# Float products of an attention stage as four column tiles of 32 outputs

## Chip, cores and metric

The kernel runs on one core of one Trainium2 chip. The metric is the device time of one launch in microseconds; the time before is the median of three runs. All data are float32, except the operands of the two 3x3 convolutions, which are 8-bit floats.

## What is computed

Two layers run one after the other on x of shape (4, 128, 128, 128), channels second. The first is a windowed attention with a convolutional feed-forward part:

```
tok = 16x16 regions of x, step 14, as rows of 128 channels
y = LN(tok);  q, k, v = split(y @ w_qkv)              # 4 heads of 32
o = softmax(q k^T / sqrt(32)) v                       # inside each region
xf = average over overlaps of (o @ w_out + b_out + tok)
y = LN(xf) @ w_p0 + b_p0                              # 128 -> 256
y = depthwise 5x5 (y);  y = gelu(gelu(batchnorm(y)))
x1 = y @ w_p2 + b_p2 + xf                             # 256 -> 128
```

The second is quantise, 3x3 convolution, batch normalisation, quantise, 3x3 convolution, batch normalisation, plus x1.

## The kernel before

**Stages.** The attention stage covers the layer norms, the attention, the projection to 256 channels and most of the depthwise convolution; it fills about the first 2240 us of the profiled span. A rest of the depthwise convolution follows, then the stage with the gelus, the second projection (L1228) and the first 3x3 convolution, and the last stage with the second 3x3 convolution (both at L1164). Engines are scheduled by hand: except on GpSimd, instructions run in the order in which the program issues them.

**Tiling of the attention stage.** The image rows are cut into 36 bands (4 images, 9 bands of 16 rows with a step of 14), and each band into 9 regions of 16x16 pixels. Channels lie on the 128 partitions. The outer loop runs over the bands `t`, the inner over the regions `j`. In each `j` the kernel issues, in this order:

- `scores(j)` (L784): per head, keys as weights of 32 rows and 128 columns, queries moving, then an exponential on ScalarE (L792);
- `values(j - 1)` (L847, L855): per head, values as weights of 128 rows and 32 columns, exponentials moving; then sums with a matrix of ones, also 32 columns wide. The four heads write to four groups of 32 PSUM partitions;
- side work, handed out by `beside(t)` in four lists: the variance of the layer norms (L377, ones of 32 columns as weights, four slices of pixels to four partition groups), the projections, and the depthwise convolution (`depthwise`, L600, weights of 40 rows and 32 columns, eight at a time);
- on every second `j`, `values_in(j)` (L770): pixels as weights of 128x128, the value part of `wqkv` moving with 128 columns. Up to four such products fill one PSUM tile `pm`, which ScalarE copies to `v` (L775).

**The projections.** `project` in `ln1_chunks` (L493) makes queries and keys of band `t + 1` or a later one: weights of 128x128, 512 or 384 pixels moving, evicted by ScalarE to `q` (L500) or `kr` (L498). `project` in `post_chunks` (L545) applies the output weights to the finished band `t - 1`, with its sum on VectorE (L546). `p0` (L561) makes the 256 channels in two halves, evicted by ScalarE to `y` (L566) and stored to DRAM for the depthwise convolution.

All of these share one PSUM pool `ps_m` of three buffers, named `pm`. The scores use a pool of two tiles and the values one tile of their own.

**Numbers of products in a run.** L493 and L561 run 288 products each, L545 144, L770 648. In the profile each float32 product leaves two MATMUL and two LDWEIGHTS records.

A second, safe form of the attention stage stands behind a flag that the program works out from the weights; it is not run with the inputs used here.

Of the kernel before, what the change touches and what calls it, by code (L numbers as in the profile page):

```python
# [14 lines left out]
P = 128  # L15
# [31 lines left out]
def layers(  # L47
# [29 lines left out]
    nc = tc.nc  # L77
# [44 lines left out]
    wqkv = const.tile([P, 3 * P], F32, name="wqkv")  # L122
    nc.sync.dma_start(out=wqkv, in_=w_qkv)
    g1, b1 = vector(ln1_g, "g1"), vector(ln1_b, "b1")
    wo = const.tile([P, P], F32, name="wo")
# [3 lines left out]
    wp0 = const.tile([P, 2, P], F32, name="wp0")  # L129
# [6 lines left out]
    with (  # L136
# [21 lines left out]
        for w in (wqkv, wp0.rearrange("p h m -> p (h m)")):  # L158
            n = w.shape[1]
# [25 lines left out]
    with ExitStack() as actx:  # L185
# [21 lines left out]
        xb, xr, yr, qs, kr, ob = {}, {}, {}, {}, {}, {}  # L207
# [218 lines left out]
        def store(out, in_):  # L426
            stores.append((out, in_))

        def flush(n, engine=nc.sync):
            for out, in_ in stores[:n]:  # L430
                engine.dma_start(out=out, in_=in_)
            del stores[:n]

        def rows_of(t, r, n):
            return t[:, r : r + n, :].rearrange("p r c -> p (r c)")

        def windows(a, n):

            a = a[:, : n * P]
            return bass.AP(a.tensor, a.offset, [a.ap[0], [STEP, NR], [P, n], [1, RS]])  # L440
# [10 lines left out]
        def row_blocks(t):  # L451
            return row_chunks(0 if bands[t][1] == 0 else 2, RS, LB)

        def load_ahead(t, n):

            if t + 1 < len(bands):
                nxt = row_blocks(t + 1)[n]
                xb[t + 1, nxt[0]] = load_rows(xp, "xt", t + 1, *nxt)

        def ln1_begin(t):  # L460
            b, i = bands[t]
            qs[t] = yp.tile([P, RS, P], F32, name="q")
            if i:
                nc.gpsimd.tensor_copy(rows_of(qs[t], 0, 2), rows_of(qs[t - 1], RS - 2, 2))
            for held, name in ((yr, "yr"), (kr, "kr")):
                held[t] = yp.tile([P, NR, RS, RS], F32, name=name)
                if i:
                    nc.gpsimd.tensor_copy(
                        held[t][:, :, 0:2, :], held[t - 1][:, :, RS - 2 :, :]
                    )  # L470

        def ln1_chunks(t, sel=None):

            chunks = []
            for at, (r, n) in enumerate(row_blocks(t)):
                held = {}
                squares, variance, deviation, spread, scaled = normalise(
                    lambda r=r, n=n: xb[t, r][:, : n * P], n * P, sel
                )

                def second(r=r, n=n, at=at, held=held, scaled=scaled):
                    held["xn"] = scaled()
                    load_ahead(t, at)
                    for hh in range(2):
                        nc.gpsimd.tensor_copy(
                            yr[t][:, :, r + hh * n // 2 : r + (hh + 1) * n // 2, :],
                            windows(held["xn"][hh], n // 2),
                        )

                def project(m, hh, r=r, n=n // 2, held=held):  # L490
                    r = r + hh * n
                    pm = ps_m.tile([P, 512], F32, name="pm")
                    nc.tensor.matmul(  # L493
                        pm[:, : n * P], wqkv[:, m * P : (m + 1) * P], held["xn"][hh],
                        start=True, stop=True,
                    )
                    if m:
                        nc.scalar.copy(kr[t][:, :, r : r + n, :], windows(pm, n))  # L498
                    else:
                        nc.scalar.activation(  # L500
                            rows_of(qs[t], r, n), pm[:, : n * P], AF.Identity, bias=qb
                        )

                chunks.append(
                    [squares, variance, deviation, spread, second]
                    + [lambda p=project, m=m, hh=hh: p(m, hh) for hh in range(2) for m in range(2)]
                )
            return chunks
# [12 lines left out]
        def finished(t):  # L521
            return row_chunks(0, RS if bands[t][1] == NR - 1 else STEP, LB)
# [5 lines left out]
        def post_chunks(t, sel=None):  # L528


            b, i = bands[t]
            chunks = []
            for at, (r, n) in enumerate(finished(t)):
                held = {}
                squares, variance, deviation, spread, scaled = normalise(
                    lambda n=n, held=held: held["xf"][:, : n * P], n * P, sel
                )

                def project(hh, r=r, n=n, at=at, held=held):
                    if hh == 0:  # L540
                        held["xf"] = xfp.tile([P, LB * P], F32, name="xf")
                    px = slice(hh * n // 2 * P, (hh + 1) * n // 2 * P)
                    pm = ps_m.tile([P, 512], F32, name="pm")
                    po = pm[:, : n // 2 * P]
                    nc.tensor.matmul(po, wo, rows_of(ob[t], r + hh * n // 2, n // 2), start=True, stop=True)  # L545
                    nc.vector.scalar_tensor_tensor(  # L546
                        held["xf"][:, px], po, bo, xr[t, at][:, px], ALU.add, ALU.add
                    )
                    if hh:
                        store(  # L550
                            xf_d[b][:, (i * STEP + r) * P : (i * STEP + r + n) * P],
                            held["xf"][:, : n * P],
                        )

                def second(held=held, scaled=scaled):
                    held["xn"] = scaled()

                def p0(h, hh, r=r, n=n // 2, held=held):
                    row = i * STEP + r + hh * n
                    pm = ps_m.tile([P, 512], F32, name="pm")  # L560
                    nc.tensor.matmul(  # L561
                        pm[:, : n * P], wp0[:, h, :], held["xn"][hh], start=True, stop=True
                    )
                    y = y2t[h].pop(0)
                    y2t[h].append(y)
                    nc.scalar.activation(  # L566
                        y[:, :n],
                        pm[:, : n * P].rearrange("p (r c e) -> p r e c", r=n, e=2),
                        AF.Identity, bias=bp0[:, h : h + 1],
                    )  # L570
                    store(
                        y2_d[b][row + 2 : row + n + 2, :, h * P : (h + 1) * P, :].rearrange(
                            "r e p x -> p (r e) x"
                        ),
                        y[:, :n].rearrange("p r e x -> p (r e) x"),
                    )

                chunks.append(
                    [lambda p=project: p(0), lambda p=project: p(1), squares, variance, deviation, spread, second]
                    + [lambda p=p0, h=h, hh=hh: p(h, hh) for hh in range(2) for h in range(2)]  # L580
                )
            return chunks
# [166 lines left out]
        def attention(t):  # L749
# [11 lines left out]
            def region(src, j):  # L761
                return src[t][:, j].rearrange("p r c -> p (r c)")

            def values_in(j):

                two = range(j, min(j + 2, NR))
                pv = ps_m.tile([P, 2, 2, P], F32, name="pm")
                for m in range(len(two)):
                    for c in range(2):
                        nc.tensor.matmul(  # L770
                            pv[:, m, c, :], region(yr, j + m)[:, c * P : (c + 1) * P], wqkv[:, 2 * P :],
                            start=True, stop=True,
                        )
                v = attn_v.tile([P, 2, 2, P], F32, name="v")
                nc.scalar.copy(v[:, : len(two)], pv[:, : len(two)])  # L775
                for m in range(len(two)):
                    S["v", j + m] = v[:, m]
# [99 lines left out]
            if safe:  # L877
                return scores_safe, lambda j: None, values_in, values
            return scores, halves, values_in, values

        def beside(t, sel=None):
# [180 lines left out]
    with (  # L1062
# [20 lines left out]
        for m in range(2):  # L1083
            for h in range(2):
# [3 lines left out]
                    start=True, stop=True,  # L1088
# [274 lines left out]
def conv_seq_kernel(tc: tile.TileContext, *args: bass.AP):  # L1363
    nc = tc.nc
    with tc.tile_pool(name="flag", bufs=1) as fp:
        flag = fp.tile([1, 1], mybir.dt.int32, name="flag")
        layers(tc, False, flag, *args)


        large = nc.values_load(flag[0:1, 0:1])  # L1370
        with tc.If(large > 0):
            layers(tc, True, flag, *args)
# [34 lines left out]
```

## Time and profile before

| | |
|---|---|
| median of three runs | 3264.07 us (3260.51 to 3272.7) |
| span of the profiled execution | 3262.4 us |
| mean granted TensorE clock | 0.965 |
| TensorE busy (MATMUL) | 3089.8 us |
| TensorE weight loads busy | 1544.8 us |
| VectorE, ScalarE, GpSimd busy | 2018.7, 1991.5, 837.6 us |
| instructions | 75,716 |
| moved by DMA | 680.65 MB, mean 209 GB/s |

The profiled execution is a run of its own; its span runs from its first to its last instruction, and lies 1.7 us under the median of the timed runs. The matmul and weight-load records of TensorE are listed as two rows, PE and PEld. A matmul's end is modelled, so that a record's length holds some time after its stream: the distance between the starts of two records says more than the length of one. "Idle before" is time in which an engine had nothing running; a releaser is what ended it. A weight shape is given as rows*columns.

### The profile page before, as it was taken

To read this page: it belongs to the slowest core of one execution; us is meant where nothing else is said; L and a number is where in the kernel's file an instruction comes from. 1 tells how busy PE (TensorE), PEld (TensorE's weight loads), DVE (VectorE), ACT (ScalarE), POOL (GpSimd) and SP (SyncE) were. 2 spreads that over 40 slices of the span, in tenths; PEclk is the share of its full clock that TensorE was granted. 3 is DMA by queue.
4 is the path that set the end of the run, shared out by engine and by line. 5 is a ranking of instruction groups with operands and counts; after the bars stand their busy time and mean duration, and the time that the engine had idled before them with its cause. 6 is when DMAs were issued, how large, how long until landed. Compare 5 with 4: busy or idle time off the path is not lost.

```text
span 3262.4 us, 75716 instructions
## 1 busy us (share of the span) xinstructions
PE 3089.8 (95%) x30954; PEld 1544.8 (47%) x30954; DVE 2018.7 (62%) x3244; ACT 1991.5 (61%) x2658; POOL 837.6 (26%) x1058
## 2 busy tenths in 40 slices
PE   8999999999999999999989998876899999999998
PEld 4555554544544444544444444443544444444443
DVE  5877887776766667676655564542555555666543
ACT  5777776777776776767655564532467777433443
POOL 3444443333333333333322232211111111000000
PEclk9999999999999999999999998877699999999999
DMA  3555677888886888886889988857899999552398
GB/s 82 150 165 159 170 185 183 192 210 198 208 200 160 193 202 204 197 209 166 188 203 207 201 199 187 191 158 199 245 359 358 357 359 306 169 167 84 106 357 312
DMA packets 809828, 680.65 MB, mean 209 GB/s; under 512 B 580919, under 2 KB 695936, under 8 KB 809472
## 3 DMA queue, kind: packets, MB, share of 16 engines
q1 hardware_dynamic: 798879, 669.17, 75.6%
q8 instruction: 247, 4.05, 0.5%
q0 software_dynamic: 1024, 3.93, 0.4%
q10 hardware_dynamic: 9568, 2.61, 0.3%
q14 instruction: 110, 0.89, 0.1%
HBM read 408.72 MB, written 270.79 MB: 208 GB/s over the span
## 4 chain that ended last, share of the span: by engine, by line
PE 80%; DMA 7%; issue 4%; ACT 4%; SPq 3%; DVE 3%; POOL 0%; ACTq 0%; DVEq 0%; POOLq 0%
PE pc L1164 21%; PE pm L600 9%; PE sc L784 9%; PE po L847 8%; PE pm L493 7%; PE pb L1228 7%; PE pm L561 5%; PE pm L770 4%; PE po L855 4%; DMA y_d<-y 3%; PE pm L377 3%; PE pm L545 3%; ACT pt L792 2%; DVE rd L867 1%; DMA u<-y_d 1%
## 5 line engine op out<-in xcount | busy, mean ns | idle before, releaser
L867 DVE RECIPROCAL rd<-po 128x256 f32<-128x256 f32 x324 | 569.3, 1757 | 447.6 <-PE po L855 444.7
L792 ACT ACTIVATE pt<-sc 128x1024 f32<-128x1024 f32 x648 | 628.0, 1024 | 128.2 <-PE sc L784 62.6
L1164 PE MATMUL pc<-q,wq 128*128 128x512 fp8e4 x3168 | 699.0, 380 | 5.1 <-DVE q L1176 5.1
L802 POOL TENSOR_TENSOR sm<-pt 128x512 f32<-128x512 f32 x324 | 413.2, 1275 | 1058.2 <-ACT pt L792 718.3
L1164 PEld LDWEIGHTS <-wq 128*128 128x128 fp8e4 x3168 | 308.7, 97 | 405.7 <-issue 37.0
L784 PE MATMUL sc<-q,kr 32*128 32x256 f32 x5184 | 403.3, 414 | 22.5 <-ACT pt L792 22.2
L600 PE MATMUL pm<-u,w 40*32 40x504 f32 (+5 forms) x7680 | 372.0, 505 | 45.6 <-DMA u<-y_d 22.5
L784 PEld LDWEIGHTS sc<-q,kr 32*128 32x128 f32 x5184 | 249.6, 190 | 261.8 <-issue 166.7
L847 PE MATMUL po<-pt,v 128*32 128x256 f32 x5184 | 358.9, 396 | 5.5 <-DVE part L871 4.7
L647 ACT COPY c<-pm 128x512 f32<-128x512 f32 (+1 forms) x256 | 132.3, 563 | 280.2 <-PE pm L600 249.4
L561 PE MATMUL pm<-xn,wp 128*128 128x512 f32 (+1 forms) x576 | 250.1, 565 | 38.1 <-ACT y L566 37.5
L566 ACT ACTIVATE y<-pm,vectors 128x512 f32<-128x512 f32 (+1 forms) x288 | 182.9, 641 | 152.4 <-DMA y_d<-y 98.3
L802 DVE TENSOR_TENSOR sm<-pt 128x512 f32<-128x512 f32 x324 | 243.7, 752 | 29.8 <-ACT pt L792 29.8
L600 PEld LDWEIGHTS pm<-u,w 40*32 40x32 f32 x7680 | 146.4, 112 | 229.9 <-issue 163.3
L493 PE MATMUL pm<-xn,wqkv 128*128 128x512 f32 (+1 forms) x576 | 248.5, 560 | 2.7 <-ACT v L775 2.0
L651 DVE BATCH_NORM_STATS2 st<-c 128x6 f32<-128x512 f32 (+2 forms) x320 | 160.9, 550 | 142.1 <-ACT c L647 141.7
L1228 PE MATMUL pb<-cv,wp 128*128 128x512 f32 x512 | 232.8, 598 | 4.9 <-ACT cv L1219 4.9
L847 PEld LDWEIGHTS po<-pt,v 128*32 128x32 f32 x5184 | 139.2, 111 | 177.9 <-issue 102.8
L1172 DVE BATCH_NORM_STATS2 st<-pc 128x6 f32<-128x512 f32 x256 | 165.8, 690 | 83.4 <-PE pc L1164 83.4
L855 PE MATMUL po<-sm,ones 128*32 128x256 f32 x2592 | 204.1, 386 | 0.8 <-issue 0.8
L770 PE MATMUL pm<-wqkv,yr 128*128 128x128 f32 x1296 | 192.8, 290 | 0.0
L770 PEld LDWEIGHTS pm<-wqkv,yr 128*128 128x128 f32 x1296 | 158.5, 191 | 67.6 <-issue 44.0
(157 smaller groups left out, 3438.3 us busy)
## 6 DMA issues: line engine op xcount, KB each, us to landing
cv<-cv_d SPq DMA_DIRECT2D x64, 1024.0 KB
u<-y_d SPq DMA_DIRECT2D x234, 256.0 KB
cv_d<-c SPq DMA_DIRECT2D x192, 256.0 KB
y_d<-y SPq DMA_DIRECT2D x160, 256.0 KB
xn<-row SPq DMA_DIRECT2D x76, 512.0 KB
xfl<-xf_d SPq DMA_DIRECT2D x64, 512.0 KB
id_d<-y SPq DMA_DIRECT2D x64, 512.0 KB
idt<-id_d SPq DMA_DIRECT2D x64, 512.0 KB
```

The costliest lines, as they stand in the source:

```text
L493: nc.tensor.matmul(pm[:, : n * P], wqkv[:, m * P : (m + 1) * P], held["xn"][hh], start=True, stop=True,)
L561: nc.tensor.matmul(pm[:, : n * P], wp0[:, h, :], held["xn"][hh], start=True, stop=True)
L600: nc.tensor.matmul(outs[half][32 * q : 32 * q + 32, j, :, a:z], wt[hs, s, c, :], ut[hs, :, c, a + s - 1 : z + s - 1], start=(s == 1), stop ...
L770: nc.tensor.matmul(pv[:, m, c, :], region(yr, j + m)[:, c * P : (c + 1) * P], wqkv[:, 2 * P :], start=True, stop=True,)
L784: nc.tensor.matmul(sc[h // 2][:, h % 2, kc, :].rearrange("p (r c) -> p r c", c=RS), region(kr, j)[hs, kc * P : (kc + 1) * P], queries(j, h ...
L792: nc.scalar.activation(pt, sc[p], AF.Exp)
L802: add(sm, pt[:, :, 0, :], pt[:, :, 1, :], ALU.add)
L847: nc.tensor.matmul(po[hs, 0, :], v[:, kc, hs], pt[h // 2][:, h % 2, kc, :], start=(kc == 0), stop=(kc == 1),)
L855: nc.tensor.matmul(po[hs, 1, :], ones, sm[h // 2][:, h % 2, :], start=True, stop=True)
L867: nc.vector.reciprocal(rd, po[:, 1, :])
L1164: nc.tensor.matmul(pc[:, h], w[:, t, :], q1[b][:, r + dy : r + dy + RB, dx : dx + P], start=(t == 0), stop=(t == 8),)
L1228: nc.tensor.matmul(pb[:, m], wp2[:, h, :], cv[:, h, px], start=(h == 0), stop=(h == 1))
```

## The change

A helper `product` issues a product of 128 outputs as four matmuls. Each takes 32 columns of the weights, the whole moving operand and 32 of the output's PSUM partitions. The four sites L493, L545, L561 and L770 call it in place of one `nc.tensor.matmul`. Moving operands, PSUM tiles, evictions, DMAs and the order of steps stay as they are. The second projection (L1228), the 3x3 convolutions and the selector products at the beginning and end of the stage (L404) are not touched.

```diff
+        def product(out, w, v):
+
+            for q in range(4):
+                m = slice(32 * q, 32 * q + 32)
+                nc.tensor.matmul(out[m], w[:, m], v, start=True, stop=True)
+
...
                     pm = ps_m.tile([P, 512], F32, name="pm")
-                    nc.tensor.matmul(
-                        pm[:, : n * P], wqkv[:, m * P : (m + 1) * P], held["xn"][hh],
-                        start=True, stop=True,
-                    )
+                    product(pm[:, : n * P], wqkv[:, m * P : (m + 1) * P], held["xn"][hh])
...
-                    nc.tensor.matmul(po, wo, rows_of(ob[t], r + hh * n // 2, n // 2), start=True, stop=True)
+                    product(po, wo, rows_of(ob[t], r + hh * n // 2, n // 2))
...
-                    nc.tensor.matmul(
-                        pm[:, : n * P], wp0[:, h, :], held["xn"][hh], start=True, stop=True
-                    )
+                    product(pm[:, : n * P], wp0[:, h, :], held["xn"][hh])
...
-                        nc.tensor.matmul(
-                            pv[:, m, c, :], region(yr, j + m)[:, c * P : (c + 1) * P], wqkv[:, 2 * P :],
-                            start=True, stop=True,
+                        product(
+                            pv[:, m, c, :], region(yr, j + m)[:, c * P : (c + 1) * P], wqkv[:, 2 * P :]
                         )
```

## The prediction

> **What bounds the kernel now.** I read the page's busy sums and the chain of waits first, then the table by windows, and last the timeline of TensorE (PE) inside the attention loop.
>
> Busy sums, and shares of the chain that ended last:
>
> ```profile
> PE 3089.8 (95%) x30954; PEld 1544.8 (47%) x30954; DVE 2018.7 (62%) x3244; ACT 1991.5 (61%) x2658; POOL 837.6 (26%) x1058
> ...
> PE 80%; DMA 7%; issue 4%; ACT 4%; SPq 3%; DVE 3%; POOL 0%; ACTq 0%; DVEq 0%; POOLq 0%
> ```
>
> TensorE is busy almost throughout and ends last for 80% of the chain; no other engine passes 62%. The windows (stretch, length, then busy time of each engine, clock share, DMA share, GB/s) cut the attention stage where its character changes:
>
> ```profile
> 300.00:1580.00 1280.00, 1256.23 (x14469) 634.31 (x14472) 918.35 (x1406) 919.60 (x1380) 478.84 (x603) 1.00 0.80 191
> 1580.00:2120.00 540.00, 490.55 (x6416) 247.95 (x6399) 299.67 (x494) 302.74 (x466) 140.15 (x179) 0.92 0.87 197
> 2120.00:2340.00 220.00, 157.07 (x3584) 107.22 (x3576) 81.46 (x274) 66.31 (x110) 30.80 (x52) 0.70 0.70 186
> ```
>
> From 300 to 1580 us PE stands still for 24 of 1280 us: a nanosecond saved there has every chance of shortening the run. After 1580 us it idles for 9% and then 29%, the transfers are busier, and the granted clock is below full.
>
> "Busy" covers more than streaming, so the timeline decides what a product costs. Start and length in us, line, output and inputs, rows*columns of the weights, moving shape, number of records:
>
> ```profile
> 1002.31 0.61 PE L855 MATMUL po<-sm,ones 128*32 128x256 f32 x8
> 1002.74 0.61 PE L377 MATMUL pm<-xf,ones 128*32 128x256 f32 x8
> 1003.17 0.61 PE L377 MATMUL pm<-sq,ones 128*32 128x256 f32 x8
> 1003.72 1.16 PE L770 MATMUL pm<-wqkv,yr 128*128 128x128 f32 x8
> 1004.71 3.68 PE L493 MATMUL pm<-xn,wqkv 128*128 128x512 f32 x8
> 1008.23 1.88 PE L545 MATMUL pm<-ob,wo 128*128 128x512 f32 x4
> 1010.04 1.15 PE L784 MATMUL sc<-q,kr 32*128 32x256 f32 x16
> 1011.12 1.07 PE L847 MATMUL po<-pt,v 128*32 128x256 f32 x16
> ```
>
> A float product leaves two records, so x8 at L855 is four column tiles. Compare starts, not lengths. L855 begins at 1002.31 and the next group at 1002.74: eight records of 256 columns in 0.43 us, that is two rounds of 216 ns with four tiles side by side. An untiled record of 512 columns at L545 follows its predecessor after 429 ns. Streaming is 0.84 ns a column in both forms, for the same 128 outputs.
>
> The differences lie at the changes of shape. From L377 at 1003.17 to L770 at 1003.72 it is 0.55 us for rounds worth 0.43: 0.12 lost. L770's eight records of 128 columns take 0.99 us; the record starts are 112 ns apart, except the first pair, 213 ns apart, because its second weights were not loaded ahead. L545's four records take 1.81 us for 1.72: 0.09 lost on the way to the scores.
>
> **What the Trainium skill says.** "TensorEngine Tiling (Array Packing)", Key Properties: changing the tiling mode, not merely the tile, drains TensorE. The trace agrees: 116 ns (median of 217) from 128x32 to 128x128, 96 ns (191) from 128x128 to the scores' 32x128. "TensorE: Matmul & The Clock Gate", LDWEIGHTS: load time goes with the number of columns, not of rows. The trace agrees: the second round after a change comes 107 ns late with 128 columns of weights, 27 ns with 32. The same page, Part 3: tiles on different column groups run concurrently, starting a few ns apart. Here the starts are 7 ns apart. Part 1 of that page says that an insufficiently busy array is throttled to half clock; the clock records show such stretches of 3 to 14 us from 1580 to 2225 us.
>
> **The change, part by part.** The float products are L493 (288), L545 (144), L561 (288) and L770 (648), 1368 in all, 2736 records. Each becomes four, so 8208 MATMUL and 8208 weight loads are added. No DMA, no eviction and no buffer is added or moved; SP, POOL, ACT and DVE keep their instructions and their order.
>
> (1) *Entering the products.* The order of records gives 220 changes from 128x32 to 128x128; after the change three remain (the selector products at start and end). Each removed entry saves the 116 ns drain and the 107 ns first load, less the 3 ns that any round costs over its stream in either place: 217 x 217 ns = 47 us gained.
>
> (2) *Leaving them.* The scores and the depthwise products have shapes of their own, so a change remains, now from column tiles. Leaving 128x32 costs 116 ns instead of 96: (191 + 27) x 20 ns = 4.4 us lost.
>
> (3) *Weights exposed between products.* When a product waits for a buffer that ACT or DVE empties, its weight load waits too. Inside runs of products some 200 records start 60 to 250 ns late, most often by 84 or 107 ns. With 32 columns a load shows 27 ns instead of 107: 200 x 80 ns = 16 us. Where ACT paces the evictions the next wait swallows it; I count half, 8 us, with ends 0 and 16.
>
> (4) *The stream itself.* Two rounds of four tiles replace two records at the same 0.84 ns a column: nothing. Nothing hides this; it rests on tile rates of L855 and L377, whose tiles read different moving slices. Bounds: see the first rival.
>
> (5) *L770's short records.* Four load-and-multiply pairs must be issued per 107 ns round. The depthwise products with 126 columns (2273 us) run eight pairs in 210 ns, an issue-bound 26 ns a pair, so four need 105 ns: just under the stream. I take nothing. The low end is a gain of 3 us (1296 records, 112 to 110 ns), the high end a fifth on 138 us of streaming, 28 us lost.
>
> (6) *What is queued behind.* The 4 x 7 ns stagger ends each product some 20 ns later for the eviction; the next product covers that. If ACT were the pacer, 1368 x 20 ns = 27 us would be the most. No wait is added. 16,416 instructions at 65 bytes each (4.94 MB of instruction transfers for 75,716) are 1.1 MB on top of 680 MB: nothing.
>
> Sum on PE: 47 - 4.4 + 8 = 51 us. Of the 217 entries 181 lie before 1580 us, so 42 us of the sum does; PE being 98% busy there, I let nine tenths through, 38 us. Of the other 8 us, where PE already waits for transfers, four tenths: 3 us. **41 us** in all. The span is 3262.4 us and the median of the runs 3264.07, 1.7 us more: against the median, 3223 us. A difference of 0.5%, 16 us, is about what a measurement of this kernel can tell from no change.
>
> **Rivals.**
> *One operand, four readers (slower).* All four tiles of a product read the same addresses at nearly the same time. Every concurrent group in this trace reads different slices, so nothing shows that this runs at full rate; that 4 and 8 tiles on arbitrary slices do speaks for it. The streams concerned are 2 x 218 us (L493, L561: 320 records of 427 ns and 256 of 320 ns each), 109 (L545) and 138 (L770): 684 us. If the tiles took turns completely that is 3 x 684 = 2052 us more, about 5300 us; two at a time, 3950 us. The point from which it decides: streams 41/684 = 6% longer cancel the gain, 8% longer make the kernel slower by 0.5%. A tenth longer gives 3291 us.
>
> *PE is quicker, something else takes the time.* For it: DMA shares of 0.80 and 0.87, waits of PE for the depthwise input (22.5 us) and of ACT for stores of y (98.3 us), and a clock that halves when PE idles; some five more such stretches of 6.8 us would cost 17 us. Against: DVE and ACT at 72% from 300 to 1580 us, where most of the gain lies. With a third of the gain let through, 3250 us; with new half-clock stretches as well, 3267 us.
>
> *The change does not merge the shapes.* If a product's tiles still drained before and after, (1) would vanish and (2), (3) and (5) remain: between -8 and +28 us, 3256 to 3292 us. Against it: L847, L855 and L377 follow one another with different operands at 216 ns without a drain.
>
> **How the numbers follow.** The forecast 0.71, with its own range from 3205 (all of (1), (2) and the full 16 us let through) to 3245; the second rival 0.13, divided between faster and same; the first 0.11, slower; the third 0.05, mostly slower. That gives faster 0.76, same 0.09, slower 0.15. The range is 3203 to 3272: it takes in the forecast and the second rival, and leaves out the slow end of the first and third and a little below.
>
> **What will show it.** Right: 39,162 records on PE and as many loads; products with 128*32 weights; the distance from the second variance group (L377) to the value products (L770) down from 0.55 to 0.43 us; L770's work (32 records) near 0.87 us instead of 0.99; a 512-column product still every 0.86 us; PE's share of the chain still near 80%. Wrong: rounds of product tiles spaced over 460 ns at 512 columns (one operand, four readers), or rounds over 125 ns at L770 (issue), or PE idle time grown by as much as the drains shrank, or more half-clock stretches.

## The result, and the profile after

The changed kernel takes 3255.23 us (median of 7 runs, 3243.95 to 3258.83) against 3265.67 us before (7 runs): a ratio of 0.9961, with a 95% interval from 0.9945 to 0.9977. Run again on a second chip (e2 below) it was 0.9948 (0.9930 to 0.9967). It is faster, by 0.4 to 0.5%, where 41 us, 1.3%, had been forecast. The profiled execution has a span of 3248.2 us. The products' lines have become L438, the helper's; lines after it have moved by up to six.

Busy sums and the chain's shares by engine, from the page of the changed kernel:

```profile
PE 3059.6 (94%) x39162; PEld 1480.1 (46%) x39162; DVE 2014.5 (62%) x3244; ACT 1988.5 (61%) x2658; POOL 840.9 (26%) x1058
...
PE 76%; DMA 9%; ACT 5%; issue 4%; SPq 3%; DVE 2%; ACTq 0%; POOL 0%; DVEq 0%; POOLq 0%
```

The 8208 added records are there, PE is busy for 30 us less, and its share of the chain has fallen from 80 to 76%, taken over by DMA and ScalarE. The same windows as before:

```profile
300.00:1580.00 1280.00, 1249.55 (x19824) 597.79 (x19824) 919.69 (x1415) 924.13 (x1391) 482.72 (x604) 0.99 0.81 193
1580.00:2120.00 540.00, 482.94 (x8022) 238.11 (x8018) 297.68 (x493) 299.98 (x463) 138.95 (x176) 0.92 0.87 198
2120.00:2340.00 220.00, 156.88 (x3590) 100.91 (x3582) 85.88 (x276) 70.32 (x109) 32.65 (x54) 0.71 0.70 192
```

From 300 to 1580 us PE now idles for 30 us instead of 24, and its clock reads 0.99 instead of 1.00. (The same window now reaches some 17 us further into the work, because the changed kernel is ahead by then.)

The timeline of PE before, 15 us after the lines shown in the prediction, where four projections of 384 columns follow the value products:

```profile
1018.09 0.61 PE L377 MATMUL pm<-sq,ones 128*32 128x256 f32 x8
1018.63 1.16 PE L770 MATMUL pm<-wqkv,yr 128*128 128x128 f32 x8
1019.63 3.04 PE L493 MATMUL pm<-xn,wqkv 128*128 128x384 f32 x8
1022.60 1.15 PE L784 MATMUL sc<-q,kr 32*128 32x256 f32 x16
...
1025.77 0.70 PE L784 MATMUL sc<-q,kr 32*128 32x256 f32 x4 [0.59 <-ACT pt L792]
```

The same place in the changed kernel:

```profile
1005.20 0.61 PE L855 MATMUL po<-sm,ones 128*32 128x256 f32 x8
1005.63 0.61 PE L377 MATMUL pm<-xf,ones 128*32 128x256 f32 x8
1006.06 0.61 PE L377 MATMUL pm<-sq,ones 128*32 128x256 f32 x8
1006.49 1.06 PE L438 MATMUL pm<-wqkv,yr 128*32 128x128 f32 x32
1007.37 3.03 PE L438 MATMUL pm<-xn,wqkv 128*32 128x384 f32 x32
1010.33 1.15 PE L784 MATMUL sc<-q,kr 32*128 32x256 f32 x16
...
1013.53 0.70 PE L784 MATMUL sc<-q,kr 32*128 32x256 f32 x4 [0.62 <-ACT pt L792]
```

From L377 to the value products it is 0.43 us (0.54 in these lines of before), the value products take 0.88 us (1.00), and no drain shows until the scores. So the merging works as described. But the four projections of 384 columns, 2.56 us of stream, still take 2.96 us, as before (2.97). The starts of their records show why. The second projection waits for the copy of the values (ScalarE, L775) to empty a PSUM tile. After that wait its second round is 105 ns late before and 25 ns late now, which is the shorter weight load; but the wait itself is now 244 ns instead of 191.

At the end of both stretches the scores of a later region wait for an exponential: 0.62 us now, 0.59 before. At this place the gain gets through: from the L377 group to the end of that wait it is 7.47 us instead of 7.68. Where a part of the gain is lost shows only in sums over many regions.

### The profile page after: what moved, and what is told of

It is laid out like the page before. It is cut to its first block, busy times and chain, and to the rows that moved or that the text cites. A ratio compares the mean times of both kernels' runs of the same rounds, so it can differ in the third digit from the quotient of the medians.

```text
span 3248.2 us, 92154 instructions
## 1 busy us (share of the span) xinstructions
PE 3059.6 (94%) x39162; PEld 1480.1 (46%) x39162; DVE 2014.5 (62%) x3244; ACT 1988.5 (61%) x2658; POOL 840.9 (26%) x1058
## 4 chain that ended last, share of the span: by engine, by line
PE 76%; DMA 9%; ACT 5%; issue 4%; SPq 3%; DVE 2%; ACTq 0%; POOL 0%; DVEq 0%; POOLq 0%
PE pc L1164 21%; PE pm L438 16%; PE sc L784 9%; PE pm L601 9%; PE po L847 8%; PE pb L1228 6%; PE po L855 3%; DMA y_d<-y 3%; PE pm L377 3%; ACT pt L792 2%; DMA u<-y_d 2%; DMA xn<-row 1%; SPq L451 1%; SPq L431 1%; ACT v L775 1%
## 5 line engine op out<-in xcount | busy, mean ns | idle before, releaser
L784 PE MATMUL sc<-q,kr 32*128 32x256 f32 x5184 | 413.6, 417 | 27.3 <-ACT pt L792 27.1
L784 PEld LDWEIGHTS sc<-q,kr 32*128 32x128 f32 x5184 | 254.1, 191 | 286.4 <-issue 177.1
L847 PE MATMUL po<-pt,v 128*32 128x256 f32 x5184 | 364.9, 401 | 10.0 <-DVE part L871 6.9
L438 PE MATMUL pm<-xn,wp 128*32 128x512 f32 (+1 forms) x2304 | 248.1, 553 | 44.6 <-ACT y L567 42.6
L438 PE MATMUL pm<-xn,wqkv 128*32 128x512 f32 (+1 forms) x2304 | 245.3, 548 | 4.9 <-ACT v L775 3.5
L1228 PE MATMUL pb<-cv,wp 128*128 128x512 f32 x512 | 232.1, 596 | 4.9 <-ACT cv L1219 4.9
L847 PEld LDWEIGHTS po<-pt,v 128*32 128x32 f32 x5184 | 140.5, 112 | 186.5 <-issue 103.5
L855 PE MATMUL po<-sm,ones 128*32 128x256 f32 x2592 | 206.1, 389 | 0.0
L874 POOL TENSOR_TENSOR ob<-ob,part 128x32 f32<-128x32 f32 x288 | 127.2, 442 | 230.6 <-DVE part L871 224.8
L438 PE MATMUL pm<-wqkv,yr 128*32 128x128 f32 x5184 | 176.3, 273 | 1.2 <-issue 1.2
```

The source lines that it names most:

```text
L438: nc.tensor.matmul(out[m], w[:, m], v, start=True, stop=True)
L784: nc.tensor.matmul(sc[h // 2][:, h % 2, kc, :].rearrange("p (r c) -> p r c", c=RS), region(kr, j)[hs, kc * P : (kc + 1) * P], queries(j, h ...
L847: nc.tensor.matmul(po[hs, 0, :], v[:, kc, hs], pt[h // 2][:, h % 2, kc, :], start=(kc == 0), stop=(kc == 1),)
L855: nc.tensor.matmul(po[hs, 1, :], ones, sm[h // 2][:, h % 2, :], start=True, stop=True)
L1228: nc.tensor.matmul(pb[:, m], wp2[:, h, :], cv[:, h, px], start=(h == 0), stop=(h == 1))
```

## The experiments

**A ledger of PE.** "Half clock" below means stretches in which the granted clock reads 0.5. For several kernels the distance from each matmul's start to the next one's was booked to the kind of the first, over the 28 bands up to about 1550 us. The sums are exactly the length of that stretch. One profiled execution stands behind each column; differences in us:

| booked to | before again (e1) | e2 - e1: column tiles | e5 - e1: less variance | e7 - e6: column tiles, less ScalarE | e13 - e14: column tiles, more VectorE |
|---|---|---|---|---|---|
| value products (L770) | 127.2 | -16.5 | 0.0 | -14.5 | -16.4 |
| variance (L377) | 107.9 | -11.3 | -28.3 | -10.4 | -12.4 |
| sums (L855) | 136.8 | -5.3 | -0.1 | -4.9 | -6.0 |
| projections (L493, L545, L561) | 463.6 | -1.6 | +8.0 | -3.8 | +17.2 |
| scores (L784) | 291.2 | +10.5 | +1.6 | +6.8 | +8.6 |
| values (L847) | 224.0 | +0.9 | -0.6 | +1.9 | +1.2 |
| depthwise (L600) | 175.5 | +1.8 | +3.0 | -3.5 | +0.7 |
| **stretch** | 1526.3 | **-21.6** | **-16.3** | **-28.5** | **-7.0** |

Time in half clock inside it: 6.8 (e1), 17.1 (e2), 13.7 (e5), 10.2 (e6), 23.9 (e7).

The first two profiles give the same picture as e2 - e1: value products -16.7, variance -10.7, sums -4.4, projections -1.3, but scores +11.2, values +3.4, depthwise +1.1, so 33.1 us off and 17.3 us gained over the stretch, with 3.4 us of half clock before and 23.9 after.

How far can one profile stand for its kernel? The stretch took 1528.7 us in the first profile of before and 1526.3 in e1; in the changed kernel it took 1511.4, 1504.7 in e2 and 1504.9 in e10, which is the same program up to there. So a column is sure to some 2 to 7 us. Two of the profiled executions also lie well above the median of their kernel's runs: that of e6 by 16 us, that of e13 by 11 us. The last two columns are weaker evidence than the others.

**e1, e2: both kernels again, side by side.** No edit.

> The kernel before, run again so that each of its runs comes with its mean granted clock. The runs of the changed kernel show 3244 to 3259 us at clocks of 0.956 to 0.960. Theory A (the gain is there on PE and is lost again to waits of PE and to the half-clock stretches that such waits set off): the clock of before lies at 0.962 to 0.966 in most runs, so 0.005 or more above the changed kernel, which over 3260 us is at least 16 us of full-clock time. Theory B (column tiles of one operand carry a cost of their own): the clocks of the two kernels agree within 0.002.

> The changed kernel again, beside before on the same chip. Both theories: 0.996 of before, 0.994 to 0.998. Theory A: over its runs, time falls as the clock rises, near 3 us for each 0.001 of mean clock (3260 us x 0.001), and the clock is near 0.957. Theory B: no such slope is needed; the clock is near 0.963.

e1: 3257.33 us, 0.9998 (0.9985 to 1.0012), mean clock over 14 runs 0.963. e2: 3240.24 us, 0.9948 (0.9930 to 0.9967), mean clock over 10 runs 0.9605, and 0.958 in the 7 runs of the result. On the same chip the clocks differ by less than 0.003, about half of what theory A named. Time falls as the clock rises, by 1.6 us per 0.001 in e2, 2.7 in the result's runs and 2.0 in 47 runs of before: slopes of loose clouds (correlations -0.6 to -0.8), and the 14 runs of e1 alone show none (0.07). If the slope holds, the lower clock makes some 5 us between e1 and e2; that is an estimate.

Where PE's own waits grew is seen at the scores. From the view of L784, the time that PE and its weight loads sat idle ahead of it, by what ended it (us, times), e1 and then e2:

```profile
  issue: 166.3, 243
  ACT pt L792: 76.2, 98
```

```profile
  issue: 175.1, 243
  ACT pt L792: 105.2, 116
```

The second line is the exponential of the region before, which must empty the scores' PSUM tiles. Waits of PE and of its weight loads are added up here and overlap in part, so the 29 us are not all time lost; the ledger puts the scores at +10.5 us. The first pair of profiles agrees: 80.9 us before, 102.2 after, and +11.2 us in the ledger.

**e3, e4: one half of the change each.**

```
 e3: product(pv[:, m, c, :], ...) at the values; nc.tensor.matmul at L493, L545, L561
 e4: nc.tensor.matmul at the values; product(...) at L493, L545, L561
```

> Only the value products (L770) are column tiles; L493, L545 and L561 stay whole. By the changes of shape counted in the trace of before, 216 of 220 entries into 128x128 remain, only at other places: shape changes cost 176 us as before, 1 us less. Theory A, whose gain comes from merged shapes alone: 1.000 of before, 0.997 to 1.003. A theory C in which each site gains by itself through its weight loads (112 ns rounds that become 107 to 109, 27 ns instead of 107 exposed) gives 5 to 17 us less, 0.995 to 0.998.

> Only L493, L545 and L561 are column tiles; the value products stay whole. The value products then stand between column tiles on both sides: 182 entries into 128x128 and 180 exits to 128x32 beside 202 exits to the scores, 17 us more on PE than before. Theory A: 10 to 20 us slower, 1.003 to 1.006. Theory C (each site by itself): 10 to 15 us faster, 0.995 to 0.997.

e3: 3255.16 us, 0.9987 (0.9974 to 0.9999). e4: 3261.98 us, 1.0014 (1.0001 to 1.0027). The halves together would make 1.000, the whole makes 0.995: the gain belongs to the merging, as theory A has it, and theory C falls by the sign of e4. Theory A had e4 at 10 to 20 us slower, which was too much. The timeline of e4 shows the new change of shape:

```profile
1018.85 0.61 PE L377 MATMUL pm<-sq,ones 128*32 128x256 f32 x8
1019.39 1.16 PE L771 MATMUL pm<-wqkv,yr 128*128 128x128 f32 x8
1020.48 2.89 PE L438 MATMUL pm<-xn,wqkv 128*32 128x384 f32 x32
1023.30 1.16 PE L785 MATMUL sc<-q,kr 32*128 32x256 f32 x16
```

L771 now takes 1.09 us up to the next product, 0.10 more than before; the four projections take 2.82 instead of 2.97. In e4's ledger (one profile) the value products take 12.7 us more than in e1, the projections 14.0 us less. So most of the added drain was taken out of waits that the projections had anyway, and e4 loses only 5 us of the 17 counted.

**e5, e8: the same time off PE without a column tile.** The mean's products in `variance` read a quarter of their pixels; ScalarE, in lines not shown here, reads that quarter four times.

```diff
+                        u = w if m else w // 4
...
-                            ps[32 * q : 32 * q + 32, m, :w], ones, v[:, q * w : (q + 1) * w],
+                            ps[32 * q : 32 * q + 32, m, :u], ones, v[:, q * w : q * w + u],
...
```

> The kernel before, all products whole, but the mean part of each variance (L377 on x and xf) is summed over a quarter of the pixels of each slice and that quarter is read four times: 144 times two rounds of 216 or 162 ns become 105 ns or less, 32 to 41 us off PE's streaming, with no change of shape, no new column tile and no change on other engines. The outputs are not the reference's. Theory A (any time taken off PE in this stage comes back in part as waits for ScalarE, and as half-clock stretches): 13 to 22 us faster, 0.993 to 0.996, mean clock down by 0.002 to 0.003, that is the same rate of return as for the column tiles. Theory B (column tiles carry a cost of their own, which this kernel has not): 30 us or more faster, 0.991 or less, clock as before.

> The changed kernel with the mean part of each variance over a quarter of the pixels, as in the kernel before it: another 32 to 41 us off PE's streaming on top of the column tiles. The outputs are not the reference's. Theory A: the return gets smaller as PE gets shorter: 5 to 15 us faster than the changed kernel, 0.990 to 0.993 of before, clock 0.957 or less. Theory B: the full 30 us and more, 0.985 or less.

e5: 3238.26 us, 0.9946 (0.9926 to 0.9965), clock 0.9607. e8: 3224.57 us, 0.9906 (0.9885 to 0.9927), clock 0.9585. In e5, 28 us are off the variance before 1550 us and 16 us arrive (58%); for the column tiles, 35 us are off and 22 arrive (62%; 17 of 33, 52%, in the first pair). The medians of the runs say the same of e5: 17 us faster, with 36 us off PE in the whole run. This decides against theory B, which wanted 30 us or more: time taken off PE without any column tile does not arrive in full either. The loss sits elsewhere, though: at the projections (+8.0) in e5, at the scores (+10.5) with column tiles. e8 lies 0.0042 below e2's ratio, 14 us, within theory A's 5 to 15, though the two were measured on different chips. But the return did not shrink, as theory A had it: in the ledger e8 has 27.8 us less variance than e2 and is 17.5 us shorter (63%).

**e6, e7: less work on ScalarE.** Squares of half the pixels; the variance, in lines not shown here, reads that half twice.

```diff
-                nc.scalar.activation(sq[:, :n], src(), AF.Square)
+                nc.scalar.activation(sq[:, : n // 2], src()[:, : n // 2], AF.Square)
...
```

> The kernel before with less work on ScalarE: the squares of the layer norms (L371) cover half of the pixels, and the sums of squares read that half twice; 144 times 0.3 to 0.45 us less on ScalarE, some 55 us, PE's work as before. The outputs are not the reference's. Theory A: PE waits for ScalarE for some 20 to 25 us in the bands up to 1550 us and the part of it that lies in the exponentials shrinks; 5 to 15 us faster, 0.995 to 0.998. Theory B: the same, it says nothing here.

> The changed kernel with the same smaller squares on ScalarE. Theory A: what the column tiles save is no longer lost behind ScalarE's queue: 28 to 40 us faster than before, 0.988 to 0.9915, and 20 to 30 us faster than the before kernel with small squares. Theory B: the difference between the two kernels with small squares stays at 13 to 18 us.

e6: 3250.41 us, 0.9979 (0.9970 to 0.9989). e7: 3229.7 us, 0.9921 (0.9903 to 0.9940). e7 lies just outside theory A's 0.988 to 0.9915. The distance is 20.7 us, at theory A's lower edge, and not to be told from e1 and e2 (17.1 us). In the ledger 33.6 us are off the products' side and 28.5 us arrive (85%), but this rests on a profile of e6 that lies 16 us above its median, and 5.3 of the 6.9 us that the stretch gains over e2 - e1 lie at the depthwise products. The scores' waits for exponentials, from 30 to 1550 us, rise as much as without the relief: from 46.3 to 67.8 us, against 47.4 to 66.7 in e1 and e2. So taking work off ScalarE in this form did not remove that wait, and whether it raises the share that arrives stays open.

**e9: half of the squares on GpSimd**, an attempt at a better complete kernel.

```diff
...
+                nc.gpsimd.tensor_tensor(sq[:, n // 2 : n], src()[:, n // 2 :], src()[:, n // 2 :], ALU.mult)
```

> The changed kernel with the second half of each layer norm's squares (L371) computed on GpSimd (x times x) instead of ScalarE; all outputs are complete. ScalarE loses the same work as with the small squares, GpSimd (56% free) gains 144 products of 384 or 512 columns, near 1.3 us each by its sums row, 190 us. Theory A: like the changed kernel with small squares, 0.990 to 0.994 of before, so 5 to 12 us better than the column tiles alone, unless the wait for GpSimd's own queue eats it. Rival: the half on GpSimd comes later than ScalarE's did, and the variance on PE (L377) waits for it: no better than the column tiles alone, 0.994 to 0.999, with L377 waiting for GpSimd by 10 us or more.

3242.84 us, 0.9956 (0.9938 to 0.9974): no better than the column tiles alone, so the rival holds. From the view of tile sq, the idle time of engines ahead of the instructions that write or read it, by what ended it (us, times):

```profile
  DVE xf L550: 73.4, 71
  POOL sq L372: 45.0, 21
```

The first line is the squares waiting for their input, the second the products of the variance waiting for GpSimd.

**e10: idle products in the late part.** One overwritten product ahead of each depthwise step of the last bands.

```diff
+                if n >= 2:
+                    m = min(3 * P, nj * ng * CW)
+                    product(pc[0].rearrange("p j g x -> p (j g x)")[:, :m], ident, wqkv[:, :m])
```

> The changed kernel with one idle product (four column tiles of 256 or 384 columns of constants, overwritten by what follows) ahead of each of the 64 depthwise steps of the late part, from 1530 us on; 40 us of added streaming on PE. It asks whether PE and its half clock set the time there. If PE sets the pace: 30 to 45 us slower than the changed kernel, 1.004 to 1.009 of before. If transfers set the pace: within 10 us of the changed kernel, 0.993 to 0.998 of before, with fewer or shorter half-clock stretches between 1550 and 2100 us (99 us of them in the changed kernel) and a mean clock above 0.962. If the half clock itself costs time there: faster than the changed kernel, 0.992 or less.

3247.82 us, 0.9967 (0.9955 to 0.9980), 7.6 us over e2 on another chip; mean clock over 11 runs 0.9644, against 0.9605 in e2. By the ledger's rule the idle products, with what they wait, take 66 us, and the late part grows by 6.4 us. The windows of e2 and then e10:

```profile
1550.00:2100.00 550.00, 494.39 (x8144) 239.16 (x8140) 309.63 (x508) 306.76 (x472) 145.02 (x185) 0.92 0.87 200
```

```profile
1550.00:2100.00 550.00, 509.64 (x8440) 239.57 (x8432) 307.69 (x505) 305.77 (x471) 145.01 (x184) 0.94 0.87 197
```

Half-clock time in this window falls from 91 to 68 us (68 and 78 us in the two profiles of before, 85 in the first of the changed kernel), and the kernel is not faster for it. Since 66 us of products cost 6 to 8 us, PE has slack after 1550 us: neither its work nor its clock sets the pace at these steps.

**e11, e12: five shared buffers for y**, two instead of three for depthwise weights.

```diff
-        y2t = [[y2p.tile([P, RB, 2, CW], F32, name=f"y2_{h}{n}") for n in range(2)] for h in range(2)]
+        y2t = [y2p.tile([P, RB, 2, CW], F32, name=f"y2_{n}") for n in range(5)]
...
```

> The changed kernel with five shared buffers for y (two for each half before), paid for by two instead of three buffers of depthwise weights. ScalarE then waits less for the stores of y (112 us in the profile of the changed kernel), and PE less for ScalarE at L561 (43 us on PE and 70 us on its weight loads). Theory A: 5 to 15 us faster than the changed kernel, 0.990 to 0.994 of before, clock up by 0.001 or more. If those waits are covered, or fewer weight buffers cost as much: 0.994 to 0.997.

> The kernel before with the same five shared buffers for y and two of depthwise weights. Theory A: it gains less than the changed kernel does, 0 to 8 us, 0.9975 to 1.000, because PE, when slower, waits less for ScalarE; the difference between the two kernels with five buffers grows to 18 to 28 us. If the buffers have nothing to do with what the column tiles lose: the difference stays at 13 to 18 us.

e11: 3240.79 us, 0.9940 (0.9917 to 0.9963). e12: 3265.57 us, 1.0012 (1.0001 to 1.0024). The changed kernel gains nothing that can be told from zero, and its clock (0.9577 over 6 runs) is lower than in e2, not higher; before loses a little. The distance between the two is 24.8 us, inside theory A's 18 to 28, but not for its reason: the changed kernel did not gain, before lost, and with some 8 us to either side the distance takes in the 17.1 us of e1 and e2. In the late part L561 is 17 to 20 us shorter in both and the depthwise products 20 to 26 us longer, so that the wait seems to have moved; two profiles of the same kernel differ by 8 to 12 us at the depthwise products. Which of the two buffer changes did that was not separated.

**e13, e14: the copy of the values on VectorE.**

```diff
-                nc.scalar.copy(v[:, : len(two)], pv[:, : len(two)])
+                nc.vector.tensor_copy(v[:, : len(two)], pv[:, : len(two)])
```

> The changed kernel with the copy of the values out of PSUM (L775) on VectorE instead of ScalarE: 180 copies, some 100 us less on ScalarE, about as much more on VectorE (72% busy until 1550 us). All outputs are complete. If ScalarE's queue takes the gain: 8 to 20 us faster than the changed kernel, 0.988 to 0.9925 of before. If the half-clock stretches take it, or VectorE's queue takes ScalarE's place: 0.993 to 0.998, no better than the column tiles alone.

> The kernel before with the same copy on VectorE. If ScalarE's queue takes the gain of the column tiles: 0 to 8 us faster than before, 0.9975 to 1.000, and the distance to the changed kernel with the same copy grows from 17 us to 25 us or more. If not, both move alike and the distance stays at 13 to 20 us.

e13: 3342.04 us, 1.0248 (1.0229 to 1.0266). e14: 3357.05 us, 1.0284 (1.0261 to 1.0307). Both ratios lie far outside every range named: the copy queues on VectorE, and PE's weight loads stand behind the PSUM buffers. The largest wait of PE's weight loads for another engine in e13; in e2 it is 25.5 us:

```profile
PEld pm L438 <- DVE rstd L384: 155.8, 136, 2.6
```

The distance between the two kernels is 15.0 us, in the 13 to 20 that e14 named for the case that ScalarE's queue is not what takes the gain. In the ledger 35 us off PE before 1550 us leave 7 us (20%), and the projections take 17 back; but e13's profile lies 11 us above its median, and the medians do not show a smaller return than e1 and e2 do.

## Why the prediction was wrong

The direction and the first two steps were right; the size was not: 41 us forecast, 10 and 17 us measured.

- **Steps (1) and (2), right.** 181 entries at 217 ns less 3.6 us of longer exits made 35.7 us before 1550 us. The ledger shows 33.1 us on values, variance and sums and 1.6 us on the projections: 34.7 us (33.1 in the first pair). About 3 us of this are the value products' rounds, 109 ns instead of 112, which belong to step (5).
- **Step (3), wrong.** It should have brought some 7 us there; after (1) and (2) nothing is left for it. The weight load does show 25 ns instead of 105 after a wait, as forecast, but at the place shown the wait for the eviction has grown by 53 ns, the exit costs the 20 ns of step (2), and four products of 384 columns stay at 2.96 us. The low end, 0, was the value.
- **Step (4), right.** Four tiles of 512 columns on one operand take two rounds of 430 ns, and the rival of one operand with four readers is out.
- **Step (5), right in its number by luck.** The 210 ns round of eight tiles at 2273 us was read as the rate at which pairs can be issued, 26 ns each. It lies in a stretch of 82 us in which the clock reads 0.50. In the same trace, at full clock, such a round of 126 columns takes 107 ns (median of 6), 13 ns a pair. So nothing there showed a limit near 105 ns for four pairs, and its high end of 28 us had no ground.
- **"Nine tenths let through" before 1550 us: the step that failed.** The share was taken from PE being 98% busy. What arrives is 62% in one pair of profiles and 52% in the other, some 10 to 13 us less than nine tenths; what step (3) did not bring makes another 7 to 8 us of the miss (estimates from the ledger). Most of the rest is found again at the scores, which take 10.5 and 11.2 us more, with more waiting for the exponentials of the region before. e5, without column tiles, returns 58%, so the low share is not peculiar to column tiles. What would raise it is open: e6 and e7 (ScalarE relieved) and e13 and e14 (VectorE loaded) stand 20.7 and 15.0 us apart, neither of which can be told from 17.1.
- **"Four tenths" after 1550 us, not shown.** The late part (bands 28 to 35 and the rest of the depthwise convolution) took 770.6 us in e1 and 776.9 in e2, 778.0 and 780.3 in the first pair of profiles. No gain shows, but the two profiles of before differ by 7.4 us, so that the 3 us forecast could not be seen. e10 gives a reason to expect none: PE has slack there.
- **The second rival** gave 3250 us with a third of the gain let through, and came closest, at a chance of 0.13. Two of the signs that the prediction named for being wrong came in part: PE's idle time grew, and there are more half-clock stretches. Before 1550 us these are 10.3 us longer in e2 than in e1 and 20.5 us in the first pair, which costs at most half of that, 5 and 10 us. In e2 the scores are 10.5 us longer, 3.8 of it in half clock. How much is lost to waits at full clock and how much to the clock was not separated.

## To carry to other kernels

Issue a 128-wide float product as four column tiles when its neighbours on TensorE are column tiles: the stream costs the same, and the drain and the exposed weight load at the change of shape go. Convert all products of the run at once, since half of them gained little (e3) or lost (e4). An engine that is 98% busy is not thereby the pace: before crediting a saving in full, take the same time off that engine in some other way and see how much of it arrives. Look at the clock record of a place, too, before reading a rate from it.

## What the runs showed of the hardware

Four column tiles that read the same moving operand ran as fast as four that read different ones: rounds of 430 ns for 512 columns, starts 6 to 8 ns apart. In a stretch of half clock streaming takes twice as long: rounds of 126 columns on eight tiles take 210 ns there and 107 ns at full clock. Such a stretch is still no proof of lost time: in e10 they were shortened without gain. One of 82 to 89 us at clock 0.50 lies over the last depthwise products in both kernels; what it costs was not tested.

Within one execution all stretches begin at one phase of a period of 3.41 us, and that phase differs between executions. The same wait can so be followed by half clock in one execution and not in another: the kernel before waits 1.3 us ahead of the scores near 525 us both in its first profile and in e1, and only in e1 a stretch of 3.4 us at half clock follows (526.5 us). That the phase decides this is an inference; no run here sets the phase.
